# Tokens dealt to tiles in interleaved groups of 32; latents and FFN inputs transposed in blocks

## The chip, the cores and the metric

The kernel runs on one core of a Trainium2 chip. The metric is the device time of one execution in microseconds (us). Three executions of the kernel before took 2807.11 us in the median (2806.98 to 2809.87).

## The reference, cut to what matters

The input is 8 batches of 512 tokens with 512 features, in fp32. The layer is a multi-head latent attention and a gated FFN, each behind a layer norm and each with a residual:

```
x = x + attention(layernorm(x));  x = x + ffn(layernorm(x))

q  = rmsnorm(h @ wq_a.T, q_norm_w) @ wq_b.T    # latents of 384, then 16 heads of 128 (nope) + 64 (rope)
kv = h @ wkv_a.T                               # 128 latents, rms-normed, + 64 rope features shared by all heads
scores = (q_nope . k_nope + rope(q_pe) . rope(k_pe)) / sqrt(192);  p = softmax(scores);  out = (p @ v) @ wo.T
ffn(y) = (silu(y @ gate_w8 * gs) * (y @ up_w8 * us)) @ down_w8 * ds      # 512 -> 1536 -> 512, weights rounded to fp8 values
```

The rotation (rope) and the softmax need the tokens' places; the other operations work on each token alone, so that it is free in which order a tile holds its tokens, as long as every reader knows it.

## The kernel before, in words

A tile has 128 partitions. A batch is held as four token tiles (128 tokens each); in the kernel before tile t holds the tokens 128t to 128t+127 in order.

**Attention.** The outer sequence is 512 steps, one for each (batch b, head h, query tile t). A step makes one tile of scores (`scores`, L427 to L448): on TensorE a matmul of the key latents `lat` with the head's query `qn` (L429, fp32) and two of the rope parts (L431, fp32r), on VectorE the row maximum (L433), on ScalarE the exponential (L436), and one step later on VectorE the reciprocal, the scaling and a transpose in blocks of 32x32 of the 128x512 probabilities (L440, L441, L443). Two tiles' blocks go together to DRAM and come back in five DMAs on SP's queue (`transposed`, L450 to L458: one write to `way`, four reads into `prT`), by which the 32x32 blocks reach their partitions and the transpose is whole. Four to five steps after a head's last scores `attend` (L460) multiplies `prT` by the key latents `kvt`, and `output` (L474) projects four heads at a time and adds to x.

The latents of the next batch are made beside this (`latents`, L299 to L390): layer norm statistics on VectorE, transposes of the centred input on TensorE (L148), the projection (L327), rms norms, the scaling of each token tile (`scale`, L349), and then for each token tile four TensorE transposes of 128x128 into PSUM (`transpose_l`, L357: L360 three times, L361 once) and one ScalarE copy into `lat` (L362). `prepare(b)` (L527) deals these pieces out over the steps of the batch before, two steps apart, from step (b-1, 5, 0) on. It loads the four tiles of x in four DMAs (L195). For batch 0 all of it runs ahead of the first step.

**FFN.** After the attention of all batches the FFN runs batch by batch (L603). For each of 12 slices i of the hidden size there are 16 matmuls (L617), then SiLU, product and a split in a high and a low fp32r part; then for each token tile 24 matmuls of the down projection (L641). The normed input of the next batch is made in the same loop (`ffn_normed`, L151): statistics at i = 4, two tiles normed at i = 6 and 8, and at the token tiles t = 0 and 1 of the down projection two times eight TensorE transposes (L148), each tile's four followed by a ScalarE copy (L175, high part `yh`) and a VectorE subtraction (L176, low part `yl`).

All DMAs are on SP's queue. The steps only give a priority: the framework's scheduler lays down the fixed order in which each engine's instructions stand. Buffers come from pools with a fixed number of slots for each tag: a new tile waits until the oldest of its tag is free.

Of the kernel before, what the change touches and what calls it, by code (L numbers as in the profile page):

```python
# [41 lines left out]
P = 128  # L42
# [18 lines left out]

def round_e4m3fn(nc, out, w, pool):
# [22 lines left out]
class Layer:  # L85
# [24 lines left out]
    def load_w(self, name, src=None, pool=None, tag=None):  # L110
        src = self.ins[name] if src is None else src
        t = (pool or self.wp).tile(list(src.shape), F32, tag=tag or name, name=name)
        self.nc.sync.dma_start(t, src)
        return t
# [36 lines left out]
    def ffn_normed(self, x, small, work, psum, bufs=None):  # L151
# [3 lines left out]
        yh = self.xp.tile([P, NC, S], F32R, tag="lat", name="yh")  # L155
        yl = self.wp.tile([P, NC, S], F32R, tag="tok", name="yl")
        got = {}

        def stats():
            moments, deviation, *got["ln"] = self.ln_stats(x, small)  # L160
            for t in range(NT):
                moments(t)
            deviation()

        def apply(t):
            mv, rstd = got["ln"]
            got[t] = work.tile([P, H], F32, tag="xn", name="xn", bufs=bufs)
            nc.vector.tensor_scalar(
                got[t], x[:, t, :], mv[:, t, 0:1], rstd[:, t : t + 1], ALU.subtract, ALU.mult
            )  # L170
# [7 lines left out]
        return stats, apply, transpose, (yh, yl)  # L178

    def attention(self):  # L180
        tc, nc, ins, wp, xp = self.tc, self.nc, self.ins, self.wp, self.xp
        with ExitStack() as ctx:
# [8 lines left out]
            def load_x(src):  # L191

                x = xp.tile([P, NT, H], F32, tag="x", name="x")
                for t in range(NT):
                    nc.sync.dma_start(x[:, t, :], src[:, t, :])  # L195
                return x

            def hidden(b):
                return ins["hid"][b].rearrange("(t p) h -> p t h", p=P)
# [3 lines left out]
            nc.sync.dma_start(x[:, 0, :], hidden(0)[:, 0, :])  # L203
            for c in range(NC):
                nc.sync.dma_start(wlr[:, c, :], ins["wlr"][:, c, :])
            for t in range(1, NT):
                nc.sync.dma_start(x[:, t, :], hidden(0)[:, t, :])
# [9 lines left out]
            def load_q(h):  # L217
                g, j = divmod(h, G)
                fold["q", h] = (
                    self.load_w("wqn", ins["wqn"][g][:, j], fp), self.load_w("wkn", ins["wkn"][g][:, j], fp)  # L220
# [4 lines left out]
            def load_o(h):  # L225
                g, j = divmod(h, G)
                fold["o", h] = (
                    self.load_w("wv", ins["wv"][g][:, j], fp), self.load_w("wo", ins["wo"][g][:, j], fp)
# [57 lines left out]
            def rope(pe, scale):  # L286

                out = sp.tile([P, S], F32, tag="tmp", name="roped", bufs=3)
                sw = sp.tile([P, S], F32, tag="tmp", name="rope_sw", bufs=3)
                own = sp.tile([P, S], F32, tag="tmp", name="rope_own", bufs=3)  # L290
# [427 lines left out]
```

## Time and profile before

| | |
|---|---|
| median of 3 runs | 2807.11 us |
| the profiled execution: time, span of its trace | 2809.15 us, 2807.4 us |
| busy: TensorE (PE), weight loads (PEld), VectorE (DVE), ScalarE (ACT), GpSimd (POOL) | 2781.0, 1578.3, 1680.4, 913.7, 349.8 us |
| share of the 16 DMA engines' time in packets of the program's queue | 39.9% |
| attention's steps, FFN | about 50 to 2271 us, 2271 to 2807 us |

How to read it: a row of a group gives line, engine, operation, result<-operands by the names of the tiles, shapes and count, then the busy time and the mean time of one. TensorE's records overlap, since matmuls are pipelined, so the start-to-start distance in the chain of waits, not the mean of one record, is what a matmul costs. Idle time stands behind the bar with what ended it. A fp32 matmul of 128x512 shows as two records.

### The profile page before, as it was taken

How to read it: one execution, taken by the hardware profiler on the slowest of the kernel's cores; microseconds unless marked ns; L12 is line 12 of the kernel's file. 1: busy time of each engine (PE TensorE's matmuls, PEld its weight loads, DVE VectorE, ACT ScalarE, POOL GpSimd, SP SyncE). 2: the span in 40 equal slices, each digit the busy share in tenths (PEclk: the TensorE clock that was granted, in tenths of full speed). 3: DMA queues.
4: the chain of work that ended last, by engine and by line, in shares of the span. 5: the costliest groups of instructions: out<-in, count | busy, mean ns of one | idle time of the engine just before them, and what ended most of it. 6: DMA issues, size and time to landing. Idle time of an engine off the chain costs nothing.

```text
span 2807.4 us, 27005 instructions
## 1 busy us (share of the span) xinstructions
PE 2781.0 (99%) x8608; PEld 1578.3 (56%) x8608; DVE 1680.4 (60%) x3528; ACT 913.7 (33%) x1928; POOL 349.8 (12%) x341
## 2 busy tenths in 40 slices
PE   7999999999999999999999999999999999999999
PEld 4555445444544454445444544554444468888887
DVE  5756676776686767666766676666666623333332
ACT  3333333333332333233333333333232223232222
POOL 2000101210020011100200011000000022222222
PEclk9999999999999999999999999999999999999999
DMA  4644454444445534453445344533555520000000
GB/s 137 195 120 139 134 165 128 140 147 157 122 137 150 172 103 146 146 165 116 138 140 170 117 139 145 157 120 116 151 174 161 155 103 30 34 31 34 30 35 19
DMA packets 229965, 345.18 MB, mean 123 GB/s; under 512 B 26048, under 2 KB 181824, under 8 KB 227136
## 3 DMA queue, kind: packets, MB, share of 16 engines
q1 hardware_dynamic: 229824, 343.46, 39.9%
q8 instruction: 69, 1.13, 0.2%
q14 instruction: 72, 0.59, 0.1%
HBM read 182.93 MB, written 160.43 MB: 122 GB/s over the span
## 4 chain that ended last, share of the span: by engine, by line
PE 98%; DVE 1%; ACT 1%; DMA 0%; POOL 0%; issue 0%; SPq 0%; ACTq 0%; POOLq 0%; DVEq 0%
PE wo_ps L482 16%; PE sc L429 16%; PE av L465 15%; PE qn_ps L401 11%; PE sc L431 8%; PE pd L641 6%; PE pu L617 6%; PE pg L617 6%; PE qpe_ps L395 6%; PE lr_ps L327 4%; PE ln_pt L148 1%; PE wvo_ps L260 0%; PE lat_pt L360 0%; PE wa_ps L245 0%; DMA x<-in_hid 0%
## 5 line engine op out<-in xcount | busy, mean ns | idle before, releaser
L436 ACT ACTIVATE pr<-sc,nmax 128x512 f32<-128x512 f32 x512 | 351.3, 687 | 781.6 <-DVE nmax L433 585.4
L431 PE MATMUL sc<-kpe,qpe 128*128 128x512 f32 x1024 | 530.4, 597 | 0.3 <-DVE qpe L413 0.3
L429 PE MATMUL sc<-lat,qn 128*128 128x512 f32 x1024 | 523.4, 593 | 2.3 <-ACT qn L403 1.9
L433 DVE TENSOR_REDUCE nmax<-sc 128x1 f32<-128x512 f32 x512 | 349.8, 684 | 256.5 <-PE sc L431 254.0
L482 PE MATMUL wo_ps<-wvo,o 128*128 128x512 f32 x1024 | 464.7, 594 | 3.5 <-ACT o L468 3.2
L465 PE MATMUL av<-prT,kvt 128*128 128x512 f32 x1024 | 461.2, 592 | 0.0
L443 DVE STREAM_TRANSPOSE block<-pr 128x512 f32<-128x512 f32 x512 | 358.4, 705 | 10.3
L401 PE MATMUL qn_ps<-lat,wa 128*128 128x512 f32 x768 | 352.5, 592 | 0.0
L431 PEld LDWEIGHTS sc<-kpe,qpe 128*128 128x128 f32 x1024 | 194.2, 190 | 246.2 <-issue 235.0
L465 PEld LDWEIGHTS av<-prT,kvt 128*128 128x128 f32 x1024 | 192.4, 190 | 216.0 <-issue 206.8
L482 PEld LDWEIGHTS wo_ps<-wvo,o 128*128 128x128 f32 x1024 | 191.4, 190 | 205.5 <-issue 180.1
L429 PEld LDWEIGHTS sc<-lat,qn 128*128 128x128 f32 x1024 | 191.2, 190 | 163.0 <-issue 140.1
L441 DVE TENSOR_SCALAR pr<-pr,rden 128x512 f32<-128x512 f32 x512 | 273.4, 534 | 13.5
L401 PEld LDWEIGHTS qn_ps<-lat,wa 128*128 128x128 f32 x768 | 145.6, 190 | 160.8 <-issue 149.3
L294 POOL TENSOR_TENSOR roped<-rope_own,rope_sw 128x512 f32<-128x512 f32 x72 | 94.4, 1311 | 1073.1 <-DVE rope_sw L293 899.6
L627 DVE SCALAR_TENSOR_TENSOR fuse<-pu,us,gate 128x512 f32<-128x512 f32 x96 | 71.9, 750 | 223.9 <-PE pu L617 205.9
L631 POOL TENSOR_TENSOR fl<-fuse,fh 128x512 fp32r<-128x512 f32 x96 | 125.2, 1305 | 460.5 <-ACT fh L630 382.3
L395 PE MATMUL qpe_ps<-lat,wqp 128*128 128x512 f32 x384 | 177.0, 595 | 0.0
L440 DVE RECIPROCAL rden<-den 128x1 f32<-128x1 f32 x512 | 78.3, 153 | 164.0 <-ACT pr L436 162.1
L74 POOL TENSOR_TENSOR q_r<-raw,q_m 128x256 f32<-128x256 f32 x72 | 54.1, 752 | 872.8 <-DVE q_m L72 775.5
L641 PE MATMUL pd<-wd,fh 128*128 128x512 f32 x384 | 150.8, 393 | 0.0
L617 PE MATMUL pg<-yh,wg 128*128 128x512 f32 x384 | 149.7, 390 | 1.1 <-DVE x L485 0.8
(90 smaller groups left out, 2880.7 us busy)
## 6 DMA issues: line engine op xcount, KB each, us to landing
way<-block SPq DMA_DIRECT2D x256, 512.0 KB, 2.8
prT<-way SPq DMA_DIRECT2D x1024, 128.0 KB, 3.5
x<-in_hid SPq DMA_DIRECT2D x32, 256.0 KB, 4.8
x<-x SPq DMA_DIRECT2D x8, 1024.0 KB, 4.4
out<-o SPq DMA_DIRECT2D x32, 256.0 KB, 2.0
fx<-x SPq DMA_DIRECT2D x7, 1024.0 KB, 5.2
wo<-in_wo SPq DMA_DIRECT2D x16, 256.0 KB, 3.9
wqn<-in_wqn SPq DMA_DIRECT2D x16, 192.0 KB, 3.5
```

The lines of the kernel that those rows point to most:

```text
L395: nc.tensor.matmul(ps, wqp_s[g][:, r, pj * P : (pj + 1) * P], lat[:, r, :], start=r == 0, stop=r == NR - 1)
L401: nc.tensor.matmul(ps, wa_s[g][:, j, r, :], lat[:, r, :], start=r == 0, stop=r == NR - 1)
L429: nc.tensor.matmul(sc, qn[:, q], lat[:, NR, :], start=True, stop=False)
L431: nc.tensor.matmul(sc, qpe[:, h % 2, q], kpe[:, part, :], start=False, stop=part == 1)
L433: nc.vector.tensor_reduce(nmax, sc, AX.X, ALU.max, negate=True)
L436: nc.scalar.activation(pr, sc, AF.Exp, bias=nmax, accum_out=den)
L441: nc.vector.tensor_scalar(pr, pr, rden, None, ALU.mult)
L443: nc.vector.transpose(block[:, :, :, i : i + Q].rearrange("p c k i -> p k c i"), pr.rearrange("p (k c j) -> p k c j", c=NQ, j=Q),)
L465: nc.tensor.matmul(av, kvt[:, kt, :], prT[:, :, :, kt, :], start=kt == 0, stop=kt == NT - 1)
L482: nc.tensor.matmul(ps, o[j][:, t * P : (t + 1) * P], wvo_s[g][:, j, :], start=j == 0, stop=j == G - 1)
L617: nc.tensor.matmul(ps, w[name, i][:, c * P : (c + 1) * P], y[k][:, c, :], start=c == 0 and k == 0, stop=c == NC - 1 and k == 1,)
L641: nc.tensor.matmul(pd, f[:, i, t * P : (t + 1) * P], w["wd", i], start=i == 0 and f is fh, stop=i == NI - 1 and f is fl,)
```

## The change

Three things change together.

**The dealing of tokens.** Token `u*256 + a*64 + t*32 + i` (i below 32) now lies in tile (u, t) on partition `a*32 + i`: a tile takes every second group of 32 tokens of its half of the batch. Loads of the input and stores of the output follow this pattern in DRAM (four groups of 32 rows in place of 128 rows one after another). Everything that stands along the free dimension in the order of tokens (`lat`, `kpe`, the rotated queries, the scores' columns) stays in natural order; `qn` and `qpe` are reordered to tiles in their copies. Because keys now have the tiles' order on one side and natural order on the other, the probabilities' transpose L443 becomes two of 128x256 each (L543), and the subtraction L413 for the queries' rope part becomes two of 64x256 (L514).

**The latents of batches 1 to 7.** TensorE's transposes and ScalarE's copies (L360 to L362) are gone for them. In their place VectorE transposes each scaled tile in 32x32 blocks (`block_l`, two instructions, 128x384 and 128x128), and for each half of the batch five DMAs on SP's queue (`send`, as for `prT`) carry the blocks to `lat`. Batch 0 keeps the TensorE way.

**The FFN's normed inputs of batches 1 to 7.** They go the same way: two norms and two block transposes (128x512) for each half, five DMAs, and then for each 128 features two ScalarE copies and two VectorE subtractions of 128x256 (`split`), in place of 16 TensorE transposes, four copies and four subtractions. Statistics start at i = 2 instead of 4, norms at i = 3 to 6. The first FFN batch keeps the TensorE way; its input now comes in one DMA instead of four.

For the space this needs, `wkn` and `wv` have one buffer instead of two, rope works in place with two buffers for each tile in place of three, `way` gets six buffers instead of four, and `yl` takes the place of `wlr`.

```diff
+def tiles(rows):
+    return rows.rearrange("(u a t i) n -> u t a i n", u=2, t=2, i=Q)
+def in_tiles(v):
+    return v.rearrange("p (u a t i) -> p u t a i", u=2, t=2, i=Q)
+def tiled(v):
+    return v.rearrange("p (u t a i) -> p u t a i", u=2, t=2, i=Q)
...
+    def blocks(self, out, x, t):
+        i = t % 2 * Q
+        self.nc.vector.transpose(
+            out[:, :, :, i : i + Q].rearrange("p c k i -> p k c i"),
+            x.rearrange("p (k c j) -> p k c j", c=NQ, j=Q),
+        )
+    def send(self, out, block):
+        way = self.dram.tile([NQ, Q, NQ, NT * 2 * Q], F32, tag="way", name="way", bufs=6)
+        nc.sync.dma_start(way.rearrange("a j c x -> (a j) c x"), block.rearrange("p c k i -> p c (k i)"))
+        for c in range(NQ):
+            nc.sync.dma_start(
+                out[c * Q : (c + 1) * Q].rearrange("j a k i -> j a (k i)"),
+                way[:, :, c].rearrange("a j x -> j a x"),
+            )
...
-        yl = self.wp.tile([P, NC, S], F32R, tag="tok", name="yl")
+            self.wp.tile([P, NC, S], F32R, tag="wlr", name="yl"),
...
+    def ffn_normed_blocks(self, x, small, work):
+        y = self.wp.tile([P, 2, NQ, NC, 2 * Q], F32, tag="tok", name="y")
...
+        def apply(t):
+            xn = work.tile([P, H], F32, tag="xn", name="xn")
+            got["ln"](t, xn)
+            if t % 2 == 0:
+                got["block"] = self.wp.tile([P, NQ, NC, 2 * Q], F32, tag="cs", name="y_block")
+            self.blocks(got["block"], xn, t)
+        def send(half):
+            self.send(y[:, half], got["block"])
+        def split(c):
+            here = y[:, :, :, c, :].rearrange("p u a (t i) -> p u t a i", i=Q)
+            hi, lo = (v[:, c, :].rearrange("p (u t a i) -> p u t a i", u=2, t=2, i=Q) for v in (yh, yl))
+            for u in range(2):
+                nc.scalar.copy(hi[:, u], here[:, u])
+                nc.vector.tensor_tensor(lo[:, u], here[:, u], hi[:, u], ALU.subtract)
...
-                    nc.sync.dma_start(x[:, t, :], src[:, t, :])
+                    nc.sync.dma_start(x[:, t, :], src[t // 2, t % 2])
...
-                    self.load_w("wqn", ins["wqn"][g][:, j], fp), self.load_w("wkn", ins["wkn"][g][:, j], fp)
+                    self.load_w("wqn", ins["wqn"][g][:, j], fp), self.load_w("wkn", ins["wkn"][g][:, j], fp, bufs=1)
...
-                lat = xp.tile([P, NR + 1, S], F32, tag="lat", name=f"lat_{b}")
+                lat = xp.tile([P, 2, NQ, NR + 1, 2 * Q], F32, tag="lat", name=f"lat_{b}")
...
+                def block_l(t):
+                    if t % 2 == 0:
+                        got["block"] = hp.tile([P, NQ, NR + 1, 2 * Q], F32, tag="lblock", name="lblock", bufs=1)
+                    self.blocks(got["block"][:, :, :NR], tok[:, t, :RQ], t)
+                    self.blocks(got["block"][:, :, NR:], kvt[:, t, :], t)
+                def send_l(half):
+                    self.send(lat[:, half], got["block"])
...
-                work += [norms, call(scale, 0)]
-                work += [both(transpose_l, scale, t) for t in range(NT)]
+                work += [norms]
+                if b == 0:
+                    work += [call(scale, 0)]
+                    work += [both(transpose_l, scale, t) for t in range(NT)]
+                else:
+                    for t in range(0, NT, 2):
+                        work += [lambda t=t: (scale(t), block_l(t)), lambda t=t: (scale(t + 1), block_l(t + 1))]
+                        work += [call(send_l, t // 2)]
...
-                    nc.tensor.matmul(ps, wa_s[g][:, j, r, :], lat[:, r, :], start=r == 0, stop=r == NR - 1)
+                    nc.tensor.matmul(ps, wa_s[g][:, j, r, :], lat[:, :, :, r, :], start=r == 0, stop=r == NR - 1)
...
-                            nc.vector.tensor_tensor(
-                                qpe[other, k, :], rotated[own], qpe[own, k, :], ALU.subtract
-                            )
+                            for u in range(2):
+                                nc.vector.tensor_tensor(lo[:, u], r[:, u], hi[:, u], ALU.subtract)
...
-                    nc.vector.transpose(
-                        block[:, :, :, i : i + Q].rearrange("p c k i -> p k c i"),
-                        pr.rearrange("p (k c j) -> p k c j", c=NQ, j=Q),
-                    )
+                    for u in range(2):
+                        nc.vector.transpose(
+                            block[:, :, 2 * u : 2 * u + 2, i : i + Q],
+                            pr[:, u * S // 2 : (u + 1) * S // 2].rearrange("p (c w j) -> p c w j", w=2, j=Q),
+                        )
...
-                self.fx = load_x(self.x2[0])
+                nc.sync.dma_start(self.fx, self.x2[0])
...
-                    if b + 1 < B and i == 4:
+                    if b + 1 < B and i == 2:
                         stats()
-                    if b + 1 < B and i in (6, 8):
-                        apply(i // 2 - 3)
+                    if b + 1 < B and 3 <= i < 3 + NT:
+                        apply(i - 3)
+                        if i % 2 == 0:
+                            send(i // 2 - 2)
...
                     if b + 1 < B and t < 2:
-                        for k in (2 * t, 2 * t + 1):
-                            transpose(k)
-                            if t == 0:
-                                apply(k + 2)
+                        for c in (2 * t, 2 * t + 1):
+                            split(c)
...
-                    nc.sync.dma_start(self.out[b, t * P : (t + 1) * P, :], o)
+                    nc.sync.dma_start(tiles(self.out[b])[t // 2, t % 2], o)
```

## The prediction

> **What bounds the kernel now.** I read the page's busy times and slices first, then the chain of waits, then busy times in windows, then the chain around the instructions that go, then single groups.
>
> ```profile
> PE 2781.0 (99%) x8608; PEld 1578.3 (56%) x8608; DVE 1680.4 (60%) x3528; ACT 913.7 (33%) x1928; POOL 349.8 (12%) x341
> ...
> PE 98%; DVE 1%; ACT 1%; DMA 0%; POOL 0%; issue 0%; SPq 0%; ACTq 0%; POOLq 0%; DVEq 0%
> ```
>
> TensorE is the chain: 98% of the span. An instruction taken from TensorE is worth its own time as long as nothing else becomes late. The windows show where TensorE is not full:
>
> ```profile
> core 0: us, PE busy (x) PEld busy (x) DVE busy (x) ACT busy (x) POOL busy (x), PEclk, DMA share, GB/s
> ...
> 10.00:15.00 5.00, 2.68 (x15) 2.03 (x14) 3.14 (x11) 2.45 (x5) 1.90 (x3) 1.00 0.92 308
> 15.00:20.00 5.00, 4.67 (x10) 2.74 (x11) 0.48 (x2) 0.64 (x3) 2.04 (x3) 0.66 0.99 314
> ...
> 50.40:2200.00 2149.60, 2147.60 (x5912) 1083.28 (x5913) 1459.16 (x3127) 723.52 (x1618) 208.35 (x221) 1.00 0.47 143
> ```
>
> In the attention's steps TensorE idles 2.0 us out of 2149.6, while VectorE is busy 68% of it. The start is different: the DMA engines are 0.92 to 0.99 busy, so there the time hangs on loads. The chain there and around the transposes:
>
> ```profile
> 3.04 5.60 DMA x<-in_hid
> ...
> 15.33 5.84 PE lr_ps L327 x16
> ```
>
> ```profile
> 2311.46 5.44 PE pd L641 x24
> 2316.91 0.87 PE ln_pt L148 x8
> 2317.78 5.46 PE pd L641 x24
> ```
>
> ```profile
> 1897.91 0.46 PE sc L431 x2
> 1898.37 0.33 PE lat_pt L360 x3
> 1898.70 0.11 PE lat_pt L361
> 1898.81 3.44 PE wo_ps L482 x8
> ```
>
> The transposes stand on the chain between matmuls without a wait: 0.87 us for eight in the FFN, 0.44 us for a latent tile's four. Groups that price what is added:
>
> ```profile
> L465 PE MATMUL av<-prT,kvt 128*128 128x512 f32 x1024 | 461.2, 592 | 0.0
> L443 DVE STREAM_TRANSPOSE block<-pr 128x512 f32<-128x512 f32 x512 | 358.4, 705 | 10.3
> L413 DVE TENSOR_TENSOR qpe<-roped,qpe 64x512 fp32r<-64x512 f32 x128 | 88.3, 690 | 73.8 <-ACT qpe L412 71.2
> L80 DVE SCALAR_TENSOR_TENSOR done<-q_m,q_r 128x256 fp32r<-128x256 f32 x72 | 32.0, 444 | 1.4
> L249 DVE SCALAR_TENSOR_TENSOR wa<-wa_ps,qnw,knr 128x128 f32<-128x128 f32 x48 | 14.2, 339 | 3.4 <-PE wa_ps L245 3.4
> ```
>
> **The change part by part.**
>
> *Removed from TensorE.* FFN: two passes of eight transposes in 7 batches, 14 x 0.87 = 12.2 us. Latents: 7 batches x 4 tiles x 0.44 = 12.3 us. Together -24.5 us, all on the chain; the bound on the other side is 0, if something else were late in every one of these places.
>
> *Matmuls with a new pattern.* `lat` is now read in runs of 64 elements. `av` reads `prT` in just such runs and takes 592 ns, L429 with the plain `lat` 593 ns: 0. The reordered copy of `qn` has its like in L468, 584 ns beside 582 ns for L403: 0.
>
> *VectorE.* L443 becomes two of half the width. No transpose of that width is in the trace: between 0.42 us (L79, 128x256) and 0.705 us (no cheaper at all). I take 0.44 us (L80): 512 x (0.88 - 0.705) = 90 us. L413 in halves: 128 x (0.88 - 0.69) = 24 us. Latent blocks: 28 tiles x (0.70 + 0.34) = 29 us, from L443 and L249. In the attention 143 us on 1491 us, 1634 of 2221 us or 74%. The heaviest of 32 equal windows of 69.4 us has 52.0 us of VectorE beside a full TensorE; it gets 16 x 0.175 + 4 x 0.19 + up to 4 x 1.04 = 7.7 us, 59.7 us. TensorE covers this, with four score buffers between them; without the cover, rival C. FFN: 28 x 0.705 + 56 x 0.44 - 28 x 0.68 = +25 us on 168 us in 536 us, hidden.
>
> *SP's queue, latents.* 14 sends of five issues at 0.33 to 0.43 us are 30 us of a queue that waits 967 us for VectorE's blocks. Each send stands among the `way` and `prT` transfers, whose reader `av` has 0.0 us of idle time before it; in the changed order `av` stands 8 to 10 score tiles behind its head's last one in the heavy stretches, where before it was 5 to 8, so a delay of some us is covered. A write and its reads land in 2.8 + 3.5 us; the second half is sent 11 steps of some 4.3 us before `project` reads it. Bound 0 to +10, taken: +2 for all small stalls of the attention, the two single-buffered weights of batch 0 among them (SP then waits for their matmul with probabilities' transfers behind it).
>
> *Loads of x.* On the DRAM side a load now begins with a dimension of 4 where every transfer in the trace begins with 32 or 128. Lower bound: 128 rows of 2 KB as before, 0. Upper bound: one DMA engine for each of the four groups. At 314 GB/s for 16 engines one moves about 20 GB/s: a tile of 262 KB then takes 3.3 us instead of 0.8, three tiles 7.4 us longer. The statistics of all four tiles end in one square root (L138), which precedes the scaling of tile 0 and so TensorE's second group of projections at 15.33. In the changed order batch 1's statistics stand on VectorE between batch 0's scalings, and wait for four more such loads: up to +14 in all. I take +6: all rows of the trace have another outer dimension, and the queue is full at this place, so that any loss of spread shows. Later loads have 30 us (seven steps): 0.
>
> The Trainium skill, page "DMA: Bandwidth & Descriptors", section "Why a DMA increments its semaphore by 16 and not by 1", says that a DMA is dealt over the largest number of engines up to 16 that divides the slowest dimension of both sides, and this speaks against the change. By it all these loads and stores run on four engines and the start costs the 7.4 us at least; with it the sum below would be 1.4 us or more worse. No run here shows it yet.
>
> *Stores of out.* The same pattern. The last one ends the kernel: 0 to +2.5 us, taken +1.5. The store ahead of the next batch's load of x can make VectorE wait longer than the 17.1 / 7 = 2.4 us of now; a slice of 3.6 us with two buffers covers that: 0, at most +1 a batch.
>
> *The first FFN batch.* It keeps TensorE's transposes, but in the changed order twelve of the 16 stand in a row, where before each four had other matmuls between. There is one PSUM buffer: each four waits for the ScalarE copy (0.59, L175) and the VectorE subtraction (0.68, L176) of the four before, 1.4 us with the handovers, twice: +3 us; 0 if they come later than the others anyway, 6 with a row maximum between.
>
> *FFN order.* `y_block` has one buffer: the third block transpose waits for the first write (2.8 us), and the product of the next slice behind it is covered by the second buffer of `pu`. The split is done in the first two of four passes of 5.4 us. ScalarE is a third busy. 0.
>
> *Sum.* -24.5 + 6 + 1.5 + 3 + 2 = -12.0 us on the profiled execution's 2809.15 us (2.0 us above the median): 2797.1, as a median **2795 us**.
>
> **The rivals.**
>
> A. *Everything is hidden*, the start too: -24.5 + 3 = -21.5, 2786 us. For it: 2 KB rows stay. Against it: the full queue at the start.
>
> B. *The start eats more*: +14, the last store +2.5, and the rest as above: -24.5 + 14 + 2.5 + 3 + 2 = -3, 2804 us, no change. For it: the order of VectorE, where batch 1's statistics hold batch 0's scalings. Against it: it needs both the full loss of spread and no slack.
>
> C. *VectorE becomes the bound* (slower). If a half-width transpose costs what a full one does, 0.705 us, a window of 69.4 us gets 16 x 0.705 = 11.3 us for scores and up to 2.8 us for L413: the mean 46.6 becomes 60.7, with latents 64.9, and the heaviest 70.3 of 69.4. VectorE also waits 162 us in all (5 us a window) for the exponential in its fixed order. Then 30 windows lose 1 to 3 us: 2795 + 30 to 90, say 2855. It decides from about 0.6 us on for one half. Against it: 128x256 rows at 0.42 to 0.44 us beside 0.69 to 0.75 us for 128x512.
>
> D. *The gain goes to new waits* (slower): `av` or the score buffers wait behind latents' sends in each batch, 7 x 3 us, and B's start: 2804 + 21 = 2825 us. Against it: VectorE at 77% in the window from 50 us on already lets TensorE wait for 0.7 us only.
>
> **How the numbers follow.** Forecast 0.45, A 0.15, B 0.18, C 0.12, D 0.10. The measurement tells 0.2% (5.6 us) from no change. Forecast and A are faster: 0.60. B is within: 0.18. C and D are slower: 0.22. The range from 2782 (A without the stall of the first FFN batch, -24.5) to 2822 (B with most of D) leaves out C, part of D and little below: some 0.18. The forecast's own range is 2786 to 2801.
>
> **What would show it.** TensorE's count of matmul records falls by 224; transposes L148 keep only the centred inputs and the first FFN batch; an FFN batch takes 1.75 us less. VectorE's half transposes read 0.42 to 0.45 us, its busy time about 1850 us. The step from the x loads to the second projection group moves from 15.3 us to about 21. If the first matmul of scores still starts near 50 us, the loads kept their spread; if it starts past 62 us, B. Idle time of TensorE before L528 or L555 of more than 10 us in all would prove the cover wrong, and half transposes above 0.6 us the price.

## The result and the profile after

The changed kernel takes 2849.97 us in the median (2849.28 to 2850.98), beside 2807.58 us for the kernel before on the same chip: 1.0147 times the time before, 95% interval 1.0135 to 1.016. The prediction was 2795 us with a range up to 2822 us. It had the wrong sign, and the time lies outside the range.

The page of the changed kernel, busy times and two rows of its slices (40 equal parts of the span, in tenths):

```profile
span 2849.2 us, 27564 instructions
...
PE 2782.3 (98%) x8384; PEld 1554.3 (55%) x8384; DVE 1757.0 (62%) x4280; ACT 885.7 (31%) x1926; POOL 348.2 (12%) x341
...
PE   6999999999999999999999999999999999999998
...
DMA  3544554445454554454545454535455552112220
```

TensorE has 224 records fewer, as it should, and still the same busy time: a record also holds part of a stall, so a busy TensorE hides what it lost. The time has to be looked for in stretches. The cuts are the first matmul of scores of a batch (L429 before, L528 after) and the first `pg` of an FFN batch, in the two profiled executions:

| stretch | before, us | after, us | difference | predicted |
|---|---|---|---|---|
| start, to the first scores | 50.4 | 65.8 | +15.5 | +6 |
| attention of batches 0 and 1 | 555.3 | 550.4 | -4.9 | |
| attention of batches 2 to 6 | 1380.9 | 1400.9 | +20.0 | |
| attention of batch 7, up to the first `pg` | 284.1 | 297.7 | +13.6 | |
| whole attention | 2220.3 | 2249.0 | +28.7 | -12.3 + 2 + 3 |
| FFN, seven starts of a batch to the next | 466.7 | 459.9 | -6.8 | -12.2 |
| last FFN batch and its store | 70.1 | 74.5 | +4.4 | +1.5 |
| sum | 2807.4 | 2849.2 | +41.8 | -12 |

(One head's product with the values, 3.4 us, can fall on either side of a cut between batches, so that only sums over batches are exact.) The busy times of the changed kernel in a few of these windows (start:end, length, then busy time and count of each engine, the granted clock as a share of TensorE's full clock, the DMA engines' share, GB/s):

```profile
core 0: us, PE busy (x) PEld busy (x) DVE busy (x) ACT busy (x) POOL busy (x), PEclk, DMA share, GB/s
10.00:15.00 5.00, 4.33 (x8) 2.18 (x7) 0.88 (x2) 0.58 (x1) 0.00 (x0) 1.00 0.46 139
15.00:20.00 5.00, 2.79 (x13) 1.99 (x12) 2.15 (x5) 0.06 (x1) 0.71 (x1) 1.00 0.33 97
...
344.50:616.20 271.70, 271.70 (x736) 136.19 (x735) 196.52 (x493) 89.06 (x204) 31.17 (x34) 1.00 0.48 146
1176.20:1456.50 280.30, 276.20 (x741) 136.82 (x740) 195.60 (x499) 88.78 (x205) 30.65 (x34) 1.00 0.49 147
2017.10:2314.80 297.70, 287.73 (x733) 136.87 (x731) 177.55 (x432) 82.32 (x189) 8.83 (x7) 0.99 0.52 152
2377.90:2444.00 66.10, 66.10 (x289) 54.05 (x288) 26.41 (x45) 20.50 (x35) 15.67 (x12) 1.00 0.21 64
```

At the start the DMA engines, 0.92 to 0.99 busy between 10 and 20 us before, are now 0.33 to 0.46 busy, and yet TensorE waits. Its granted clock is lower for longer there, too: the trace has it at half for 20.5 us of the changed kernel's start and for 10.2 us of that of the kernel before. Batch 1 has no idle time; batch 4 has 4.1 us, with VectorE no busier than in batch 1 (195.6 and 196.5 us). What TensorE (PE) and ScalarE (ACT) waited for in the whole span, in us, times and the longest, after:

```profile
PE wo_ps L568 <- ACT o L557: 13.1, 14, 1.8
PE ln_pt L164 <- DVE xc L395: 11.5, 2, 9.3
PE lr_ps L407 <- ACT xT L400: 9.9, 4, 5.2
PE qn_ps L500 <- DVE x L571: 4.2, 5, 0.8
PE sc L528 <- ACT pr L535: 3.3, 6, 0.6
```

```profile
ACT pr L535 <- DVE block L543: 351.1, 94, 14.7
ACT pr L535 <- DVE nmax L532: 340.5, 167, 5.9
```

The second and third line of TensorE are the start. The others are small waits, most of them for ScalarE's copies. ScalarE itself waits 351 us, up to 14.7 at once, for VectorE's half-width transposes L543, which free the two buffers of the probabilities `pr`; before, it waited 112 us for L443, and 585 us in the normal way, for the row maximum:

```profile
ACT pr L436 <- DVE nmax L433: 585.4, 280, 5.3
...
ACT pr L436 <- DVE block L443: 112.4, 53, 8.3
```

The price of those transposes is not the reason:

```profile
L543 DVE STREAM_TRANSPOSE block<-pr 128x256 f32<-128x256 f32 x1024 | 389.0, 420 | 8.0
L514 DVE TENSOR_TENSOR qpe<-roped,qpe 64x256 fp32r<-64x256 f32 x256 | 100.1, 418 | 78.2 <-ACT qpe L512 75.0
```

Their place is. VectorE's sequence in batch 4, after (start, us, engine, line, what, and idle time ahead of it in brackets):

```profile
1188.51 0.17 DVE L539 RECIPROCAL rden<-den 128x1 f32<-128x1 f32 x1 [2.16 <-ACT pr L535]
1188.59 0.67 DVE L532 TENSOR_REDUCE nmax<-sc 128x1 f32<-128x512 f32 x1
1189.18 0.48 DVE L540 TENSOR_SCALAR pr<-pr,rden 128x512 f32<-128x512 f32 x1
1189.57 0.16 DVE L539 RECIPROCAL rden<-den 128x1 f32<-128x1 f32 x1
1189.87 0.69 DVE L532 TENSOR_REDUCE nmax<-sc 128x1 f32<-128x512 f32 x1
1190.47 0.47 DVE L540 TENSOR_SCALAR pr<-pr,rden 128x512 f32<-128x512 f32 x1
1191.19 0.69 DVE L532 TENSOR_REDUCE nmax<-sc 128x1 f32<-128x512 f32 x1 [0.24 <-PE sc L530]
1192.52 0.69 DVE L532 TENSOR_REDUCE nmax<-sc 128x1 f32<-128x512 f32 x1 [0.64 <-PE sc L530]
...
1197.39 0.75 DVE L514 TENSOR_TENSOR qpe<-roped,qpe 64x256 fp32r<-64x256 f32 x2 [2.11 <-ACT qpe L512]
1198.51 0.76 DVE L514 TENSOR_TENSOR qpe<-roped,qpe 64x256 fp32r<-64x256 f32 x2 [0.36 <-ACT qpe L512]
1199.28 1.42 DVE L543 STREAM_TRANSPOSE block<-pr 128x256 f32<-128x256 f32 x4
```

Both `pr` tiles are scaled by 1190.9 us. Their transposes come at 1199.3, behind two more row maxima, a rotation and two waits for `qpe`; only then can the next exponentials run. VectorE idles 0.2 to 2.2 us at several of these places: it isn't short of time, it stands in a worse order. Before, a transpose follows its scaling at once:

```profile
1188.36 0.16 DVE L440 RECIPROCAL rden<-den 128x1 f32<-128x1 f32 x1 [0.28 <-ACT pr L436]
1188.56 0.49 DVE L441 TENSOR_SCALAR pr<-pr,rden 128x512 f32<-128x512 f32 x1
1189.09 0.71 DVE L443 STREAM_TRANSPOSE block<-pr 128x512 f32<-128x512 f32 x1
```

Over batches 2 to 6, 1.94 later row maxima stand on average between a tile's own maximum and its last transpose (call it the lateness), and an exponential starts 4.1 us after its maximum; before, 0.74 and 0.63 us.

So there were four things to explain: the start, the order in the attention, FFN matmuls that got dearer (below), and the last store.

### The profile page after: what moved, and what is told of

Read it like the earlier page. It is cut to its first block, busy times and chain, and to the rows that moved or that the text cites. A ratio compares the mean times of both kernels' runs of the same rounds, so it can differ in the third digit from the quotient of the medians.

```text
span 2849.2 us, 27564 instructions
## 1 busy us (share of the span) xinstructions
PE 2782.3 (98%) x8384; PEld 1554.3 (55%) x8384; DVE 1757.0 (62%) x4280; ACT 885.7 (31%) x1926; POOL 348.2 (12%) x341
## 5 line engine op out<-in xcount | busy, mean ns | idle before, releaser
L528 PE MATMUL sc<-lat,qn 128*128 128x512 f32 x1024 | 523.9, 593 | 4.2 <-ACT pr L535 3.3
L568 PE MATMUL wo_ps<-wvo,o 128*128 128x512 f32 x1024 | 470.0, 596 | 17.8 <-ACT o L557 13.1
L555 PE MATMUL av<-prT,kvt 128*128 128x512 f32 x1024 | 464.2, 595 | 0.0
L543 DVE STREAM_TRANSPOSE block<-pr 128x256 f32<-128x256 f32 x1024 | 389.0, 420 | 8.0
L568 PEld LDWEIGHTS wo_ps<-wvo,o 128*128 128x128 f32 x1024 | 190.5, 189 | 234.2 <-issue 179.0
L555 PEld LDWEIGHTS av<-prT,kvt 128*128 128x128 f32 x1024 | 194.1, 191 | 222.5 <-issue 214.4
L528 PEld LDWEIGHTS sc<-lat,qn 128*128 128x128 f32 x1024 | 190.6, 189 | 154.5 <-issue 121.3
L540 DVE TENSOR_SCALAR pr<-pr,rden 128x512 f32<-128x512 f32 x512 | 258.7, 506 | 12.8
L373 POOL TENSOR_TENSOR roped<-roped,rope_sw 128x512 f32<-128x512 f32 x72 | 92.1, 1279 | 1142.5 <-DVE rope_sw L372 955.4
L571 DVE TENSOR_TENSOR x<-x,wo_ps 128x512 f32<-128x512 f32 x128 | 86.4, 678 | 153.7 <-PE wo_ps L568 153.5
L512 ACT CAST qpe<-roped 64x512 fp32r<-64x512 f32 x128 | 78.9, 617 | 239.5 <-POOL roped L373 238.0
```

Of the source, the lines that this page charges most:

```text
L528: nc.tensor.matmul(sc, qn[:, q], lat[:, :, :, NR, :], start=True, stop=False)
L540: nc.vector.tensor_scalar(pr, pr, rden, None, ALU.mult)
L543: nc.vector.transpose(block[:, :, 2 * u : 2 * u + 2, i : i + Q], pr[:, u * S // 2 : (u + 1) * S // 2].rearrange("p (c w j) -> p c w j", w= ...
L555: nc.tensor.matmul(av, kvt[:, kt, :], prT[:, :, :, kt, :], start=kt == 0, stop=kt == NT - 1)
L568: nc.tensor.matmul(ps, o[j][:, t * P : (t + 1) * P], wvo_s[g][:, j, :], start=j == 0, stop=j == G - 1)
```

## The experiments

The attention of a batch below is the mean of batches 2 to 6 in the profiled execution: 276.2 us before, 280.2 after.

**e1: plain rows.** The dealing leaves the DRAM side; on the chip all stays.

```diff
-    return rows.rearrange("(u a t i) n -> u t a i n", u=2, t=2, i=Q)
+    return rows.rearrange("(u t p) n -> u t p n", u=2, t=2)
...
-            cs_s = self.load_w("cs")
+            for k in range(2):          # the table permuted by eight DMAs
+                for u in range(2):
+                    for t in range(2):
+                        nc.sync.dma_start(in_tiles(cs_s[:, k, :])[:, u, t], tiled(ins["cs"][:, k, :])[:, u, t])
```

> The changed kernel with plain rows (tile t holds 128 neighbouring rows) in the loads of x and the stores of out, and the table of the rotation permuted to match; all work on the chip stays. Theory 1 (the dealt rows, four runs of 32 on the DRAM side, put each load and store on few DMA engines): the first scores go back from 65.8 us to 50 to 53, the last store from about 5 to about 2 us, so 2850 - 14 - 3 = 2833 (2829 to 2838). Rival (the start is late through the weights' single buffers on SP's queue): first scores stay past 62 us, 2846 to 2850.

2829.03 us, 1.007 (1.0055 to 1.0085). First scores at 48.9 us; from the last matmul to the end 4.6 us, as before, where the changed kernel has 8.2. Batch by batch the attention is that of the change (280.2 us). The gain of 21 us is a little over the expected 17. The same windows of e1, which stand against 0.46 and 0.33:

```profile
10.00:15.00 5.00, 3.13 (x17) 2.44 (x16) 3.00 (x9) 2.92 (x7) 2.36 (x3) 1.00 0.89 180
15.00:20.00 5.00, 4.45 (x20) 3.12 (x20) 1.57 (x5) 1.30 (x5) 0.97 (x2) 1.00 0.81 192
```

**e9: dealt rows, four DMAs for one.** This separates the rows from the form of the DMA; loads of batches 0 and 1, and all stores of `out`.

```diff
-                nc.sync.dma_start(x[:, t, :], hidden[0][t // 2, t % 2])
+                for a in range(NQ):
+                    nc.sync.dma_start(x[a * Q : (a + 1) * Q, t, :], hidden[0][t // 2, t % 2, a])
```

> The changed kernel with the dealt rows kept, but each load of x of batches 0 and 1 and each store of out issued as four DMAs of 32 neighbouring rows instead of one DMA with four runs. Theory 1a (a single DMA with four runs on its DRAM side is carried by few DMA engines; where the rows lie doesn't matter): first scores at 50 to 55 us (24 more issues of 0.45 us on SP, some of them ahead of the weights), the end 3 us shorter: 2850 - 14 = 2836 (2830 to 2841). Rival 1b (the dealt rows are slow in themselves): 65.8 us stays, 2846 to 2853.

2836.18 us, 1.0097 (1.008 to 1.0114): as theory 1a has it. First scores at 53.6 us, the end 5.5 us after the last matmul. So the form of the DMA, one with four runs on its DRAM side, brings 12.2 of the 16.9 us that e1 gains at the start; the other 4.7 us can be the place of the rows or the 24 more issues, which isn't separated. The Trainium skill's rule that the prediction weighed ("DMA: Bandwidth & Descriptors", section "Why a DMA increments its semaphore by 16 and not by 1") agrees with this and with the low share of 0.33 to 0.46: by it the one form runs on four engines, the other on 16.

**e2: all latents on TensorE.**

```diff
-                if b == 0:
+                if b < B:
                     work += [call(scale, 0)]
                     work += [both(transpose_l, scale, t) for t in range(NT)]
```

> The changed kernel with the latents of all eight batches transposed on TensorE, as it does for batch 0; the FFN's blocks, the dealt rows and the half-width transposes stay. Theory 2 (the latents' blocks put clumps on VectorE that make the exponentials, then ScalarE's copies of o and qn, then TensorE's output projection late): batches 2 to 6 go from 280.3 us back to 275 to 277 each although 1.76 us of transposes come back, 2850 - 20 = 2830 (2823 to 2838). Rival (the half-width transposes and the rearranging copies make the waits, which are in every batch): the waits stay and the transposes come on top, 2855 to 2862.

2826.25 us, 1.0061 (1.0046 to 1.0076). A batch takes 276.6 us; batch 7, which makes no latents, falls from 297.7 to 283.7. Theory 2's number came true, but its reason (clumps of work) is tested only by e5 and e6. The half-width transposes and the rearranging copies stay in, and cost nothing that shows (0.4 us a batch).

**e4: the half-width transposes alone**, in the kernel before.

```diff
-                    nc.vector.transpose(
-                        block[:, :, :, i : i + Q].rearrange("p c k i -> p k c i"),
-                        pr.rearrange("p (k c j) -> p k c j", c=NQ, j=Q),
-                    )
+                    for u in range(2):
+                        nc.vector.transpose(
+                            block[:, :, 2 * u : 2 * u + 2, i : i + Q].rearrange("p c k i -> p k c i"),
+                            pr[:, u * S // 2 : (u + 1) * S // 2].rearrange("p (k c j) -> p k c j", c=NQ, j=Q),
+                        )
```

> The kernel before with each 128x512 transpose of pr cut in two of 128x256, everything else as before. By the rows: 512 x (2 x 0.42 - 0.71) = 67 us more on VectorE. If VectorE's mean load is what makes TensorE wait (rival to theory 2): 2820 to 2835. Theory 2: hidden, 2806 to 2812.

2809.26 us, 1.0002 (0.9992 to 1.0011). Hidden. VectorE's load is not the bound.

**e5: the latents' sends on POOL's queue.**

```diff
-        nc.sync.dma_start(way.rearrange("a j c x -> (a j) c x"), block.rearrange("p c k i -> p c (k i)"))
+        queue.dma_start(way.rearrange("a j c x -> (a j) c x"), block.rearrange("p c k i -> p c (k i)"))
...
-                    self.send(lat[:, half], got["block"])
+                    self.send(lat[:, half], got["block"], nc.gpsimd)
```

> The changed kernel with the ten DMAs that send a batch's latents (two ways out, eight reads back) issued from POOL's queue instead of SP's; VectorE's work is the same. Theory 2a (SP's one queue in order: the latents' sends stand before the sends of the probabilities, so the sequence written for TensorE puts each head's product with the values later, 54 matmuls after its scores instead of 43, and the waits come from there): batches 2 to 6 go from 280.3 to 274 to 275 us each, the last from 297.7 to about 283; 2850 - 42 = 2808 (2800 to 2816). Rival 2b (the blocks' clumps on VectorE): batches stay near 280, 2842 to 2855.

2824.97 us, 1.0056 (1.0041 to 1.0071), 25 us gained of the 42 expected. With VectorE's work unchanged the attention falls by 28.0 us (2249.0 to 2221.0), a batch to 276.3, batch 7 to 283.4; the exponential starts 0.67 us after its maximum. ScalarE waits again for maxima, 597 us, and 119 us for transposes, about as before (112):

```profile
ACT pr L535 <- DVE nmax L532: 597.2, 266, 5.3
...
ACT pr L535 <- DVE block L543: 118.9, 54, 8.4
```

So ten DMAs a batch in SP's queue, not the blocks on VectorE, bring most of the loss. The edit moves no work, and yet the engines' sequences are written anew around it: 2620 of the 4280 places in VectorE's, and 2252 of the 8384 in TensorE's, hold another instruction than in the changed kernel. The rest is a wait of 1.2 to 2.5 us in each batch.

**e6: the blocks and their sends without their use.** TensorE makes the latents; the blocks go out and back into themselves.

```diff
-                        work += [lambda t=t: (scale(t), block_l(t)), lambda t=t: (scale(t + 1), block_l(t + 1))]
+                        work += [lambda t=t: (scale(t), transpose_l(t), block_l(t))]
+                        work += [lambda t=t: (scale(t + 1), transpose_l(t + 1), block_l(t + 1))]
...
-                    self.send(lat[:, half], got["block"])
+                    self.send(got["block"], got["block"])
```

> The changed kernel with the latents of all batches transposed on TensorE, and besides it the blocks on VectorE and their ten DMAs on SP as in the changed kernel, into the block itself, where nobody reads them: the work and the queue of the change without its use. Theory 2a or 2b: the waits of batches 2 to 6 stay and the transposes come on top, 282 us each; 2850 + 12 = 2862 (2852 to 2872). Rival 2c (TensorE waits for the latents themselves, that land later): no waits, 276 us each, 2826 to 2832.

2870.32 us, 1.0219 (1.0202 to 1.0236); a batch 283.5 us, lateness 1.98. Nobody waits for these transfers, and the loss is all there. This rules out that TensorE waits for the latents themselves.

**e3, e7, e10: the place of `yl`.** In the changed kernel a matmul of `pg` or `pu` takes 230.9 ns from start to start, before 226.7; the down projection is unchanged. The matmuls that are dearer have a fixed place in each group of eight, also in the last batch, where nothing is prepared beside them. e3 exchanges the buffers of `yl` and `y`; e7 and e10 leave `yl` in the buffer of `wlr`, 64 and 704 bytes further on.

```diff
-            self.wp.tile([P, NC, S], F32R, tag="wlr", name="yl"),
+            self.wp.tile([P, NC, S], F32R, tag="tok", name="yl"),                                          # e3
+            self.wp.tile([P, NC * S + 16], F32R, tag="wlr", name="yl")[:, 16:].rearrange(...),             # e7
+            self.wp.tile([P, NC * S + 176], F32R, tag="wlr", name="yl")[:, 176:].rearrange(...),           # e10
```

> The changed kernel with two tiles exchanged: yl back in the buffer that it had before (tok), y in that of wlr. Theory 3 (the place of yl in SBUF slows the matmuls that read yh and yl): eight matmuls of pg and pu go from 1.85 back to 1.81 us, 2850 - 7 = 2843. Rival (something else that the change moves): 1.85 us stays, 2850.

> The changed kernel with yl in the same buffer (wlr), 64 bytes further on, so that its rows begin at a multiple of 128 bytes as in the kernel before, and not 64 off it. Theory 3a (the offset): a matmul of pg and pu goes from 231 to 227 ns, 2850 - 6 = 2844. Rival 3b (the part of SBUF that the buffer lies in): 231 ns stays, 2850.

> The changed kernel with yl in the buffer of wlr, 704 bytes further on, so that its place modulo 2048 bytes is that of yh and of yl in the kernel before (384). Theory 3c (the place of yl against that of yh, modulo some power of two): a matmul of pg and pu goes back to 227 ns. Rival 3b (the part of SBUF): about 231 ns stays.

e3: 2845.47 us (1.0127, 1.0112 to 1.0143), 226.7 ns in the last batch. e7: 2850.45 us (1.0148, 1.0132 to 1.0163), 230.0 ns in the last batch, with other places of the eight dearer. e10: 2847.56 us in one run, 226.7 ns in the last batch. (In e3 and e10 every engine's sequence is that of the changed kernel.) So it is neither an offset of 64 bytes nor the part of SBUF: by the addresses in the built programs, `yl` begins at 704 and 768 bytes modulo 1024 in the two kernels with the dearer matmuls, and in the others at 384, where `yh` begins too. The expectation of e10 says modulo 2048, which is wrong: `yl` begins there at 1408 modulo 2048, so that the run shows that 384 modulo 1024 is enough. Rows of the page, the changed kernel and then e10:

```profile
L703 PE MATMUL pu<-yh,wu 128*128 128x512 f32 x384 | 152.4, 397 | 0.0
L703 PE MATMUL pg<-yl,wg 128*128 128x512 f32 x384 | 150.1, 391 | 0.0
```

```profile
L703 PE MATMUL pu<-yh,wu 128*128 128x512 f32 x384 | 151.0, 393 | 0.0
L703 PE MATMUL pg<-yl,wg 128*128 128x512 f32 x384 | 149.5, 389 | 0.0
```

Those that read `yh`, which didn't move, lose more than those that read `yl`. (In batches 1 to 6 a matmul of e3 and e10 takes 226.8 to 227.7 ns from start to start, in e8, with plain rows, 226.7. Why some are dearer there is not shown; e3 took back 4.5 us in all.)

**e8: the three together**, plain rows, `yl` in `tok`, the latents' sends on POOL's queue (the edits of e1, e3, e5).

> The changed kernel with plain rows, yl in the buffer tok and the latents' sends on POOL's queue. If the three causes are separate, their gains add: start and end -21, yl -4.5, batches -42: 2782 (2775 to 2792), 0.9% under the kernel before. Rival (they are one cause seen three times, or a new wait takes their place): 2800 to 2830.

2796.85 us, 0.9958 (0.9943 to 0.9973). Below the kernel before, but 15 us over the sum: e5's part of it had already missed 17.

**e11: the FFN's blocks alone** (the edits of e1, e2, e3).

> Plain rows, the latents of all batches on TensorE, yl in the buffer tok: of the change's two savings the FFN's blocks alone. If the causes add: 2850 - 21 - 24 - 4.5 = 2801 (2796 to 2806), 0.3% under the kernel before; the FFN's batch 65.3 us against 67.08, so 12.3 us of the 12.2 predicted for it. Rival (the blocks' waits reach TensorE in the FFN): 2808 to 2815.

2798.47 us, 0.9964 (0.9951 to 0.9977). An FFN batch takes 65.28 us against 67.08: the FFN's 12.2 us are there in full (7 x 1.80 = 12.6).

**e12: e8 with the output projection one step later.** In e8 one wait in each batch was left: the third group's projection L568 for ScalarE's copy `o` of the head just before it.

```diff
-                                later[i + n].append(f) for n, f in zip((7, 8, 11, 12, 13), output(b, g))
+                                later[i + n].append(f) for n, f in zip((8, 9, 12, 13, 14), output(b, g))
```

> The last kernel of the runs before (plain rows, yl in tok, latents' sends on POOL's queue) with the output projection of each group of four heads one step later. Theory 4 (what is left of the latents' gain is one wait per batch, the third group's projection standing right behind the last head's product and waiting 1.3 to 2.5 us for ScalarE's copy o): batches 2 to 6 from 276.3 to 274.3 us on average, 2797 - 12 = 2785 (2780 to 2790). Rival (the later projection holds o and the PSUM buffers, and a new wait takes its place): 2794 to 2806.

2788.91 us, 0.9928 (0.9914 to 0.9943): a batch 274.7 us, 1.4 us under the kernel before, where 1.76 us of transposes were taken out.

**e13 and e14: two readings of TensorE's sequence.** In the changed kernel the products with the values stand later behind their scores, and the projections are woven around them. e13 is the kernel before with products and projections two steps later; e14 is the changed kernel with the projections four steps later.

```diff
-                    later[i + 5].append(lambda b=b, h=h, prT=prT: attend(b, h, prT))        # e13
+                    later[i + 7].append(lambda b=b, h=h, prT=prT: attend(b, h, prT))
...
-                                later[i + n].append(f) for n, f in zip((7, 8, 11, 12, 13), output(b, g))
+                                later[i + n].append(f) for n, f in zip((9, 10, 13, 14, 15), output(b, g))     # e13
+                                later[i + n].append(f) for n, f in zip((11, 12, 15, 16, 17), output(b, g))    # e14
```

> The kernel before with each head's product with the values and each group's output projection two steps later, nothing else: the products then stand 52 matmuls after their head's last score in TensorE's sequence, where before it was 43 and in the changed kernel 54, and the first matmul of a group's projection 7 or more behind the last product. Theory 5a (the late products in themselves make the waits): batches 2 to 6 near 280 us, 2830 to 2842. Theory 5b (the waits come from the projection being woven around its late last product, 15 to 25 matmuls ahead of it, which holds a PSUM buffer and then waits for ScalarE's copy): no waits here, 2804 to 2814.

> The changed kernel with each group's output projection four steps later, nothing else: SP's queue is as loaded as in the change, products 60 matmuls behind their scores, but the projections begin 8 behind to 9 ahead of the last product and no more 25 ahead of it. Theory 5b: most of the waits go, batches 2 to 6 at 275 to 277 us, 2850 - 20 to -30 = 2820 to 2830. Theory 5a or 2b (late products, or the queue itself): batches stay at 280 or more, 2846 to 2865.

e13: 2804.90 us, 0.9988 (0.9978 to 0.9998); late products cost nothing. e14: 2890.89 us, 1.0296 (1.028 to 1.0311), a batch 286.6 us; its lateness is 2.54 and the exponential 7.1 us behind. Both theories fell. What runs with the loss in every kernel is VectorE's order:

| kernel | lateness, row maxima | maximum to exponential, us | batch, us |
|---|---|---|---|
| e13 | 0.47 | 0.34 | 276.2 |
| before | 0.74 | 0.63 | 276.2 |
| e2, all latents on TensorE | 0.77 | 0.64 | 276.6 |
| e5, sends on POOL's queue | 0.80 | 0.67 | 276.3 |
| after | 1.94 | 4.13 | 280.2 |
| e6, sends without use | 1.98 | 4.38 | 283.5 |
| e14 | 2.54 | 7.10 | 286.6 |

(In e13, before, e2 and e6 a batch holds 1.76 us of the latents' transposes, in the others not. In e14 the granted clock is at half for 6.1 us of a batch on average, in the changed kernel not at all in these batches, so that up to 3 of its 6.4 us more are the clock's.)

**e15: an edge on this order.** An edge of order lets no row maximum stand ahead of the transposes of the tile two before it. SP's sequence and the work stay; 408 of the 8384 places in TensorE's sequence and 271 of the 1880 in ScalarE's hold another instruction than in the changed kernel.

```diff
+                if n - 2 in turned:
+                    tc.add_manual_dep(top.ins, turned[n - 2].ins.name, ...NoSync...)   # top: the row maximum of step n
```

> The changed kernel with one order written for VectorE: the row maximum of a score tile may not stand ahead of the half-width transposes of the tile two before it (an edge of order, no work and no transfer is added). In the changed kernel 1.94 later row maxima stand on average ahead of a tile's transposes, up to 5, in the kernel before 0.75; with the edge 0.78, at most 1. TensorE's own sequence stays that of the change (products 53.6 matmuls behind their scores). Theory 6 (the late transposes keep the two pr buffers, so that exponentials come 4 us late, and from there ScalarE's copies and TensorE): batches 2 to 6 from 280.3 to 275 to 277 us, the last one shorter too; 2850 - 25 = 2825 (2815 to 2832). Rival (SP's queue itself or the work on VectorE): 2845 or more.

2839.37 us, 1.0105 (1.0089 to 1.0122): 11 us, where 25 were expected. A batch takes 279.2 us, batch 7 291.4 instead of 297.7. The exponential is again 0.63 us behind its maximum, but the maximum now comes late, in batch 4 4.7 us behind its scores, where it was 0.8: the delay has moved up the chain. In e15, ScalarE:

```profile
ACT pr L543 <- DVE nmax L532: 603.5, 249, 13.9
```

So VectorE's order is part of the mechanism, but no single pair of instructions is the whole of it: with the ten DMAs on SP's queue the written sequences of all engines are others, and only taking them out of that queue (e2, e5) sets most of it right at once.

Does the queue also delay at run time, beside the order that is written for it? The traces speak against it. From batch 2 to the first `pg` of the changed kernel no wait of VectorE, ScalarE or TensorE's matmuls above 0.15 us was ended by a DMA, and of the weight loads' waits three of 0.2 us were (GpSimd waited for one once, 15.6 us, before three times). In e6 and e15 it is the same for these engines but GpSimd. With these sequences a faster queue could hardly have helped. And batches 0 and 1 of the changed kernel send ten DMAs each on the same queue, but have a lateness of 1.0 and 1.1, and together they are 4.9 us shorter than before (1.5 if one product falls on the other side of the cut), where 3.5 us were taken out. Why the scheduler writes another order from batch 2 on is not shown.

**e16: e12 with this edge.**

> The fastest kernel of the runs before (plain rows, yl in tok, latents' sends on POOL's queue, output projections one step later; 2788.9 us) with the same edge of order on VectorE. Theory 6: its lateness falls from 0.9 to 0.56 row maxima in the batches and from 2.09 to 0.86 in the last one, so only the last batch (283 us, 4.2 idle) has something to give: 2785 to 2789. Rival (the fixed order costs waits of its own): 2792 to 2800.

2783.13 us, 0.9907 (0.9892 to 0.9921), 0.9% under the kernel before and the fastest here. Its page and two windows (batch 4, an FFN batch):

```profile
PE 2756.9 (99%) x8384; PEld 1554.8 (56%) x8384; DVE 1749.5 (63%) x4280; ACT 909.5 (33%) x1936; POOL 387.7 (14%) x411
```

```profile
1153.20:1428.20 275.00, 274.49 (x741) 137.39 (x740) 196.64 (x498) 92.54 (x207) 36.10 (x45) 1.00 0.50 149
...
2321.40:2386.70 65.30, 65.30 (x290) 54.07 (x289) 25.56 (x45) 21.00 (x35) 15.88 (x12) 1.00 0.19 65
```

The span is 2783.0 us, 24.4 under that of the kernel before, close to the -24.5 us that the transposes were priced at. In part this is luck. The FFN gives its 12.6 us. Of the 11.4 us in the attention 8.2 are in batches 0 to 6, where 12.3 were taken out, and 3.1 in batch 7, where nothing was; e13, which has the transposes, gains 3.4 us there. The later projection and the edge were not put on the kernel before, so what they would give there is not known.

## Why the prediction was wrong, by its own steps

- **Removed from TensorE, -24.5 us: right for the FFN's half.** 224 records went. The FFN's 12.2 us come in full (e11, e16); of the latents' 12.3 us the runs show 8.2 (e16, batches 0 to 6). In the changed kernel itself the gain is buried under 66 us of costs.
- **SP's queue, latents, "0 to +10, taken +2": this step failed.** Batches 2 to 7 and the first FFN batch together lost some 41 us (whole attention +28.7 instead of -12.3), of which 3 to 6 are the next step's. I asked only whether `av` would still come after its `prT`, and it does: L555 has 0.0 us of idle time. I did not ask what the five issues do to the order in which VectorE's and ScalarE's work is written. e5 gives 28.0 of the 41 us back by moving just those DMAs. The later projection (e8 to e12) takes 9.3 us more from the attention, the edge on VectorE (e12 to e16) 4.3, some of which they might have given the kernel before as well.
- **The first FFN batch, +3: right in its waits, but not the whole.** Twelve transposes stand in a row, and L164 waits three times for VectorE's subtraction L227, 3.1 us; its time from start to start grows by 3.6 us. As its last four begin, the granted clock goes to half, from 2122.0 to 2128.8 us, which costs up to 3.4 us (some 0.4 of it in the 3.6) and stood in no term; in e2 and e5 batch 7 has no such stretch. This order too goes with the latents' sends: in e2 other matmuls stand between the four groups again, and batch 7 takes 283.7 us, 0.4 less than before. The other 7 us or so that batch 7 lost belong to the step above.
- **Loads of x, "+6, bound +14": mis-sized, +15.5**, above my own upper bound. The mechanism was right: the form of the DMA (e9 takes back 12.2 us). The bound was too low by its own working: 7.4 us for three loads and 2.5 for each of four more are some 17, not 14. Two things were left out of it whose part isn't separated. The weights' issues stand behind these loads on SP's queue, and the first `wkn` is issued at 15.97 us, before at 9.30; but in e9 it is issued at 14.20, and the first scores still come 12.2 us sooner. And the granted clock is at half for 10.3 us more than before, an estimated 5 us at most (half of that); in e9 for 3.5 us more. The skill's rule, which spoke against the change, should have had the upper bound and not the middle.
- **Stores of out, +1.5: mis-sized, +3.6** (8.2 us from the last matmul to the end, before 4.6); e1 takes it back in full.
- **A term that was missing: `yl` in the buffer of `wlr`.** I counted that move as free. It costs 4.2 ns for each of 1536 matmuls of `pg` and `pu`, 6.5 us.
- **VectorE, hidden: right.** 0.42 us a half transpose (taken 0.44), VectorE 1757 us busy; I had 1850, since records overlap and their busy time grows by less than their means. e4 shows +0.02% for the half transposes alone, and in e5 VectorE has all of the change's work and a batch takes 276.3 us. Rival C is refuted.
- **Matmuls with a new pattern, 0: right** (429 ns from start to start for `av` and `qn`, before as after). **FFN order, 0: right** (e11).
- **The rivals.** D was nearest, with 2825 us: it had new waits behind the latents' sends, at 3 us a batch, and B's start. The loss was 6 us a batch and 7 to 10 in the last, and came by another way. I gave D a chance of 0.10, on the ground that a busy VectorE had let TensorE wait little; VectorE's mean load was the wrong row to read.
- **The sign I had named**, TensorE idle before L528 or L555, would have missed it: 4.2 and 0.0 us, while 17.8 stood before L568 and more inside the records. The sign for the start, first scores past 62 us, did come (65.8).

## What to carry to other kernels

A DMA that is put on a queue that a planned pipeline uses is not priced by its issue time: the fixed order of every engine is written around that queue, and a tile that keeps a double-buffered operand a few instructions longer starves the engine in front of it, though nobody waits for the DMA. That the order is written so is the scheduler's doing, and shows only when the program is built: batches 0 and 1 had the same DMAs and lost little or nothing. Before such a change, compare the written orders of all engines, not only the one that bounds; afterwards compare waits engine by engine, and try the transfers on another queue first. Look at the outermost dimension of each DMA on the DRAM side, and at where a moved buffer begins.

## What the runs showed of the hardware

- Loads of 128 rows of 2 KB in one DMA each with four runs on the DRAM side kept the DMA engines 0.33 to 0.46 busy between 10 and 20 us, with a full queue behind them; the same rows in four DMAs bring the first scores from 65.8 to 53.6 us, plain rows to 48.9.
- The place of a moved operand in SBUF changes the rate of fp32r matmuls that alternate between two operands: 230.9 and 230.0 ns in the last batch where `yl` begins at 704 and 768 bytes modulo 1024, 226.7 where it begins at 384 like `yh`, in either of two buffers. Which property of the address decides stays open.
- A 32x32-block transpose on VectorE costs by its width: 0.29 us for 128x128, 0.42 for 128x256, 0.56 for 128x384, 0.69 to 0.71 for 128x512.
- Ten DMAs a batch issued by POOL take it 0.62 us (a write out, 512 KB) and 0.56 us (a read back, 128 KB) each to issue and land 3.0 and 3.7 us after it. No cost of theirs shows in e12: a batch takes 274.7 us, where the kernel before less its transposes would take 274.4.
- In the changed kernel TensorE had three waits of 0.2, 1.5 and 1.5 us between 2118 and 2123 us, and from 2122.0 to 2128.8 us its granted clock was at half.
